# A mixture-of-experts tail in five parts: rows gathered one place ahead, more buffers, and a scaling kept in program order

## The chip, the cores and the metric

The kernel runs on one core of a Trainium2 chip. The metric is the device time of one execution in microseconds (us). Before the change it is 2043.39 us, the median of 3 runs (2043.01 to 2043.95).

A core has a matrix engine (TensorE, PE in the profile), a vector engine (VectorE, DVE), an engine for activation functions (ScalarE, ACT), a general engine (GpSimd, POOL) and a sequencer that here issues most of the transfers (SyncE, SP). Each works through its own list of instructions in order and waits on semaphores for the others. Matrix products land in PSUM, of which this kernel uses eight banks; everything else is in SBUF or in the chip's main memory.

## What is computed

Two layers on a tensor of 4 sequences of 512 positions of 512 features, all in 32-bit floats. Each layer adds an attention and a mixture of experts to its normalised input. The change lies in the second layer ("layer 1"), whose mixture is

```python
logits = einsum('bsd,de->bse', x, router_w) + router_b
topk_vals, topk_idx = top_k(logits, 2)
topk_w = softmax(topk_vals)
h = einsum('td,edf->etf', xf, expert_w) + expert_b
combined = sum over the two chosen experts of topk_w * silu(h)
out = combined @ proj_w + proj_b
y = x + out
return norm_w * y / sqrt(mean(y * y) + 1e-6)
```

and the layer's result is `x + attention(xn) + mixture(xn)`. Only the two experts chosen for a position count, so the kernel sorts the positions by expert, computes each expert on its own rows, and gathers every position's two rows back.

## The kernel before

The 2048 positions are 16 tiles of 128 rows. Layer 1's attention has 16 steps `g` (4 sequences times 4 groups of heads), each of 4 parts `kc` (128 keys each); a pair (g, kc) is called a place, and place number 4 g + kc runs from 0 to 63. In each place the loop at the end of `two_layers` writes, in this order:

- the scores (`weights`: TensorE L1322, then two exponentials on ScalarE, L1324);
- the weighted values of the place before (`attend`: TensorE L1336) and, for kc > 0, the running sums of the exponentials (VectorE L1342);
- for kc = 1 the sums over keys (`sum_keys`, L1350) and after it reciprocals (`invert`, L1360) and the scaling of the context (L1368);
- for kc < 2 the next step's queries and keys (`queries7`, L1298 and VectorE L1303 to L1313), and for kc > 1 in some steps the next sequence's values;
- `bring(n, 0)`, which reloads the partial result of a tile of an earlier sequence, and for kc = 3 that tile's output projection (`output1`, TensorE L1405), whose sum is added to it (`add_part`, VectorE L1394) and stored;
- then the jobs that a table (`jobs1`) has for this place.

Those jobs fill TensorE's time in the attention with the mixture: the routing first, the expert products in places 13 to 45 (`apply`, L529, whose result rows go to a table `yd` in main memory), and from place 48 on the last stage, which this change is about. Tile n starts at place 48 + 13 n // 16, so some places (48, 52, 56) start two tiles, and the last ends in place 63. A tile has four jobs in four places that follow each other:

- `mix`: two gathers from `yd` (`gather`, GpSimd issues them, L545) into `row0` and `row1`; the load of the normalised input `xnd` into a buffer `xr` (SP, L1435); the rows' weighted sum on VectorE (L1438, L1439); the bias `pb` added to the input on GpSimd (L1440).
- `turn_mix`: four transposes on TensorE (L1447), the reload of the tile's partial result from `accd` (`bring(n, 1)`, SP, L1390), the copy out of PSUM on ScalarE (L1451).
- `project_mix`: eight matmul records on TensorE (L1458), the sum with the input on VectorE (L1459), the squares on ScalarE (L1462), mean and power on GpSimd (L1463, L1464).
- `finish_mix`: the scaling with the norm's weight on VectorE (L1469), the addition to the partial result (L1394) and the store.

All buffers of this stage are in a pool `mix` with two buffers to a name. Products and transposes of the stage take their PSUM bank from the same three (`bank1`, name `mm`) as the queries, the output projection and the key sums.

The order in which an engine executes is not the written one. A planner goes through the program with estimated times and gives each engine, of what is ready, the instruction written first; a tile that finds no free buffer is not ready. `tc.keep_in_program_order(instruction)` pins an instruction behind the one that was written last before it on its engine. In the stage only L1438 of the first two tiles is pinned.

## Time and profile before

| | |
|---|---|
| median of 3 runs | 2043.39 us |
| profiled execution | 2039.16 us |
| its span, first to last instruction | 2037.1 us |
| TensorE busy in the span | 1983.6 us (97%) |
| VectorE busy | 1506.5 us (74%) |
| GpSimd busy | 746.3 us (37%) |
| last stage, place 48 to the last weighted values | 1860.6 to 2012.8 us of the span |

The profile is of one execution. A row of the stretch view gives the stretch and its length, then the busy time of each engine with the number of instructions, then the clock granted to TensorE as a share of full speed, the busy share of the transfer engines and their rate. A row of the view of waits gives the engine, the tile and line that waited, what ended the wait, and then the sum in us, how many times, and the longest. A row of the view in order of time gives start, duration, engine, line, operation, output and inputs, and in brackets the idle time of the engine before it with its releaser.

### The profile page before, as it was taken

What the parts mean: (1) busy time and instruction counts of PE and PEld (TensorE: products, weight loads), DVE (VectorE), ACT (ScalarE), POOL (GpSimd) and SP (SyncE); (2) the same over time, 40 slices, a digit from 0 to 9 for tenths busy, and PEclk for the clock granted to TensorE, in tenths of its full rate; (3) what the DMA queues carried; (4) which work ended last, traced back from release to release, by engine and by line L of the source; (5) the groups of instructions that cost most, each with busy time, mean ns of one, the idle gap of its engine ahead of it and who ended that gap; (6) DMA issues with size and microseconds to landing.
All of it is one profiled execution on the core that took longest, in us unless ns stands there. A gap on an engine that the chain in (4) does not pass through costs nothing.

```text
span 2037.1 us, 28573 instructions
## 1 busy us (share of the span) xinstructions
PE 1983.6 (97%) x9358; PEld 1243.6 (61%) x9358; DVE 1506.5 (74%) x3696; ACT 868.5 (43%) x2600; POOL 746.3 (37%) x761
## 2 busy tenths in 40 slices
PE   7999999999999999999999999999999999999998
PEld 4666667777777777767667666666334445445443
DVE  7889968777776777786678878788596555557775
ACT  4554444444444444444444454454244432332332
POOL 4423144443323333344343444353114332322550
PEclk8999999999999999999999999999999999999999
DMA  7101133333433343245443222121317775773551
GB/s 254 69 33 62 43 120 123 145 109 114 126 133 104 115 153 104 96 135 186 183 161 118 73 89 74 42 74 64 121 55 253 271 255 194 270 245 112 154 161 59
DMA packets 98909, 267.27 MB, mean 131 GB/s; under 512 B 14400, under 2 KB 27840, under 8 KB 87488
## 3 DMA queue, kind: packets, MB, share of 16 engines
q0 software_dynamic: 27072, 148.91, 21.6%
q1 hardware_dynamic: 70528, 114.34, 16.7%
q10 hardware_dynamic: 1152, 2.10, 0.3%
q8 instruction: 77, 1.26, 0.3%
q14 instruction: 80, 0.66, 0.1%
HBM read 222.05 MB, written 42.73 MB: 130 GB/s over the span
## 4 chain that ended last, share of the span: by engine, by line
PE 81%; DVE 9%; ACT 3%; POOL 2%; issue 2%; DMA 1%; ACTq 0%; DVEq 0%; SPq 0%; POOLq 0%
PE p L675 25%; PE hp_r L529 12%; PE op L842 4%; PE st L767 4%; PE sp L758 2%; PE st L1322 2%; PE ox L873 2%; PE qp L1298 2%; PE cx L1336 2%; PE ca L811 2%; DVE pS L1342 2%; PE o L1405 2%; PE oz L873 2%; PE trm_r L517 1%; PE trq L695 1%
## 5 line engine op out<-in xcount | busy, mean ns | idle before, releaser
L529 PE MATMUL hp_r<-we_r,xT_r 128*128 128x512 f32 (+1 forms) x592 | 224.7, 596 | 2.7 <-ACT xT_r L519 2.2
L481 POOL DMA_INDIRECT xr_r<-xnd,rows_r x72 | 87.5, 1216 | 342.2 <-PE trm_r L517 299.0
L775 POOL TENSOR_TENSOR lT<-lT,lmask 128x512 f32<-128x512 f32 (+1 forms) x128 | 152.6, 1200 | 129.1 <-ACT lT L771 128.9
L675 PE MATMUL p<-wT,x 128*128 128x384 f32 x512 | 178.7, 492 | 0.8 <-DVE wT L119 0.8
L675 PE MATMUL p<-wB,x 128*128 128x384 f32 x512 | 176.2, 488 | 3.0 <-DVE u L731 3.0
L675 PE MATMUL p<-wA,xnT 128*128 128x384 f32 x512 | 174.3, 492 | 0.3 <-DVE u L710 0.2
L575 ACT ACTIVATE sq<-qb 128x128 f32<-128x128 f32 x384 | 118.9, 310 | 96.2 <-DVE qb L724 45.8
L1324 ACT ACTIVATE pT<-st 128x1024 f32<-128x1024 f32 x128 | 123.3, 1014 | 62.5 <-PE st L1322 56.7
L529 PEld LDWEIGHTS hp_r<-we_r,xT_r 128*128 128x128 f32 (+1 forms) x592 | 83.0, 170 | 98.8 <-issue 92.5
L675 PEld LDWEIGHTS p<-wB,x 128*128 128x128 f32 x512 | 93.7, 190 | 67.1 <-issue 9.6
L675 PEld LDWEIGHTS p<-wA,xnT 128*128 128x128 f32 x512 | 95.5, 193 | 61.6 <-issue 3.3
L675 PEld LDWEIGHTS p<-wT,x 128*128 128x128 f32 x512 | 94.2, 192 | 62.7 <-issue 5.5
L689 ACT ACTIVATE qb<-qb,ss 128x128 f32<-128x128 f32 x256 | 81.9, 390 | 106.6 <-POOL ss L578 104.5
L519 ACT COPY xT_r<-trm_r 128x512 f32<-128x512 f32 x72 | 41.9, 581 | 193.4 <-PE hp_r L529 180.8
L767 PE MATMUL st<-qkT 128*128 128x256 f32 (+1 forms) x512 | 114.7, 354 | 1.5 <-ACT qkT L702 1.5
L771 ACT ACTIVATE lT<-st,ss 128x256 f32<-128x256 f32 (+1 forms) x128 | 49.0, 446 | 153.0 <-PE st L767 153.0
L545 POOL DMA_INDIRECT row_r<-yd,slot_r x64 | 75.0, 1172 | 89.8 <-DVE row_r L1439 37.6
L767 PEld LDWEIGHTS st<-qkT 128*128 128x128 f32 x512 | 92.2, 190 | 11.9 <-ACT qkT L702 1.7
L578 POOL TENSOR_TENSOR ss<-ss,nhalf 128x6 f32<-128x6 f32 x64 | 95.4, 1490 | 5.3
L842 PE MATMUL op<-Wo,cT 128*128 128x512 f32 x208 | 93.7, 595 | 0.4 <-DVE lv L739 0.4
L577 POOL TENSOR_SCALAR ss<-ss 128x6 f32<-128x6 f32 x64 | 31.0, 485 | 164.3 <-ACT sq L575 163.9
L675 PE MATMUL p<-wT,xnT 128*128 128x384 f32 x256 | 88.0, 486 | 0.0
(384 smaller groups left out, 4632.7 us busy)
## 6 DMA issues: line engine op xcount, KB each, us to landing
x<-xsd SPq DMA_DIRECT2D x112, 256.0 KB, 3.2
yd<-yr_r SPq DMA_DIRECT2D x72, 256.0 KB, 4.4
wA<-in_wA SPq DMA_DIRECT2D x16, 384.0 KB, 3.9
wB<-in_wB SPq DMA_DIRECT2D x16, 384.0 KB, 7.6
xnd<-xn SPq DMA_DIRECT2D x24, 256.0 KB, 2.1
accd<-acc SPq DMA_DIRECT2D x18, 256.0 KB, 2.0
acc<-in_x SPq DMA_DIRECT2D x16, 256.0 KB, 4.9
Wo<-in_Wo SPq DMA_DIRECT2D x8, 512.0 KB, 3.7
```

The lines of the kernel that those rows point to most:

```text
L481: G.indirect_dma_start(out=out, out_offset=None, in_=src, in_offset=at_rows(idx))
L529: PE.matmul(hp[ts(h, m), :], lhsT=xT[:, k, ts(h, m)], rhs=w[:, ts(k, HID)], start=(k == 0), stop=(k == KC - 1))
L545: G.indirect_dma_start(out=x, out_offset=None, in_=self.yd, in_offset=at_rows(self.r.slot[:, k, n : n + 1]))
L575: A.activation(sq, x[:, h, :], AF.Square, accum_out=ss[:, h : h + 1])
L578: pin(G.tensor_tensor(ss, ss, nhalf[:, 0:n], ALU.pow))
L675: PE.matmul(p, lhsT=x[:, k, ts(c, P)], rhs=w[:, k, :], start=(k == 0), stop=(k == 1))
L689: A.activation(x[:, j, :], x[:, j, :], AF.Copy, scale=sq[t][:, j : j + 1])
L767: PE.matmul(st[:, ds((t % 2) * 256, n)], lhsT=qkT[:, HG + h, ts(t, P)], rhs=qkT[:, h, ds(t * P, n)], start=True, stop=True)
L775: G.tensor_tensor(dst, dst, lmask.rearrange("p a w j -> p (a w j)")[:, 0:n], ALU.mult)
L842: PE.matmul(op, lhsT=cT[:, h, ts(t, P)], rhs=wo[:, h, :], start=(h == 0), stop=(h == HG - 1))
L873: PE.matmul(p[:, ts(c, 256)], lhsT=left[:, ts(c, P)], rhs=right, start=new and c == 0, stop=True, skip_group_check=True)
L1324: A.activation(pt[:, ts(pair, 2), :], st, AF.Exp, scale=SCALE1)
```

## The change

The stage has five jobs instead of four. The gathers become a job of their own, `fetch_mix`, one place ahead of `mix`, and the pool of the stage is opened one place earlier (place 47). `row0` has four buffers and `row1` three in this layer, `xr` four, the transposed tile (`xT`) three, the squares (`th`) one. The load of `xnd` moves from `mix` to `turn_mix`, the addition of `pb` from `mix` to `project_mix`. L1438 is pinned for all tiles, and so is L1469. The reload for the output projection, `bring(n, 0)`, is written in kc = 0 instead of kc = 1.

```diff
--- before.py
+++ after.py
@@ -541,7 +541,8 @@
 
             rs = []
             for k in range(2):
-                x = self.pool.tile([P, HID], F32, tag=f"row{k}", name=f"row{k}_{self.r.name}_{n}")
+                x = self.pool.tile([P, HID], F32, tag=f"row{k}", name=f"row{k}_{self.r.name}_{n}",
+                                   bufs=(4, 3)[k] if self.silu else None)
                 G.indirect_dma_start(out=x, out_offset=None, in_=self.yd,
                                      in_offset=at_rows(self.r.slot[:, k, n : n + 1]))
                 rs.append(x)
@@ -1428,36 +1429,38 @@
         for nm in ("pb", "nw1"):
             rows[nm] = load(rout["mix"], nm, [P, HID], a[nm].partition_broadcast(P))
 
+    def fetch_mix(n):
+
+        held[n] = rout["ex1"].gather(n)
+
     def mix(n):
 
-        g0, g1 = rout["ex1"].gather(n)
-        x = rout["mix"].tile([P, HID], F32, tag="xr", name=f"xa_{n}")
+        g0, g1 = held[n]
+        tc.keep_in_program_order(V.tensor_scalar(g0, g0, r1.gate[:, 0, n : n + 1], None, ALU.mult))
+        V.scalar_tensor_tensor(g0, g1, r1.gate[:, 1, n : n + 1], g0, ALU.mult, ALU.add)
+        held[n] = g0
+
+    def turn_mix(n):
+        g0 = held[n]
+        x = rout["mix"].tile([P, HID], F32, tag="xr", name=f"xa_{n}", bufs=4)
         nc.sync.dma_start(out=x, in_=xnd[ts(n, P), :])
-
-        pin = tc.keep_in_program_order if n < 2 else (lambda x: x)
-        pin(V.tensor_scalar(g0, g0, r1.gate[:, 0, n : n + 1], None, ALU.mult))
-        V.scalar_tensor_tensor(g0, g1, r1.gate[:, 1, n : n + 1], g0, ALU.mult, ALU.add)
-        G.tensor_tensor(x, x, rows["pb"], ALU.add)
-        held[n] = g0, x
-
-    def turn_mix(n):
-        g0, x = held[n]
         tr = bank1("mm", f"trc_{n}")
         for f in range(KC):
             PE.transpose(tr[:, ts(f, P)], g0[:, ts(f, P)], ident)
         bring(n, 1)
-        cT_ = rout["mix"].tile([P, KC, P], F32, tag="xT", name=f"combT_{n}")
+        cT_ = rout["mix"].tile([P, KC, P], F32, tag="xT", name=f"combT_{n}", bufs=3)
 
         A.activation(cT_, tr.rearrange("p (k t) -> p k t", k=KC), AF.Copy, scale=0.5)
         held[n] = cT_, x
 
     def project_mix(n):
         cT_, y = held.pop(n)
+        G.tensor_tensor(y, y, rows["pb"], ALU.add)
         op = bank1("mm", f"po_{n}")
         for f in range(KC):
             PE.matmul(op, lhsT=cT_[:, f, :], rhs=wa["pw"][:, f, :], start=(f == 0), stop=(f == KC - 1))
         V.tensor_tensor(y, y, op, ALU.add)
-        sq = rout["mix"].tile([P, HID], F32, tag="th", name=f"ysq_{n}")
+        sq = rout["mix"].tile([P, HID], F32, tag="th", name=f"ysq_{n}", bufs=1)
         ss = small.tile([P, 1], F32, tag="yss", name=f"yss_{n}")
         A.activation(sq, y, AF.Square, accum_out=ss)
         G.tensor_scalar(ss, ss, 1.0 / HID, 1e-6, ALU.mult, ALU.add)
@@ -1466,7 +1469,7 @@
 
     def finish_mix(n):
         y, ss = held.pop(n)
-        V.scalar_tensor_tensor(y, y, ss[:, 0:1], rows["nw1"], ALU.mult, ALU.mult)
+        tc.keep_in_program_order(V.scalar_tensor_tensor(y, y, ss[:, 0:1], rows["nw1"], ALU.mult, ALU.mult))
         add_part(n, y, 1)
 
 
@@ -1499,10 +1502,10 @@
             ex.fetch_bias(i + 2)
         jobs1.append((at[here], after))
     first += 6 + NS * 11 // 12
-    jobs1.append((at[first], begin_mixing))
+    jobs1.append((at[first - 1], begin_mixing))
     for n in range(NT):
         here = first + n * 13 // 16
-        for d, f in ((0, mix), (1, turn_mix), (2, project_mix), (3, finish_mix)):
+        for d, f in ((-1, fetch_mix), (0, mix), (1, turn_mix), (2, project_mix), (3, finish_mix)):
             jobs1.append((at[here + d], lambda n=n, f=f: f(n)))
 
     left_ = sums_qk()
@@ -1556,7 +1559,7 @@
             if kc > 1 and j + 1 == NJ and 1 < b + 1 < B:
                 values7(b + 1, kc - 2)
 
-            if kc == 1 and g > NJ:
+            if kc == 0 and g > NJ:
                 bring(g - NJ - 1, 0)
             if kc == 2 and g + 1 == NG:
                 bring(NT - TC - 1, 0)
```

## The prediction

> **What bounds the kernel now.** I read the page first, then the busy time of each engine in stretches of the last stage, then the waits of each queue there, and last its instructions in order of time. The page says that TensorE is the bound over the whole program: nothing can be gained where it is busy.

> ```profile
> span 2037.1 us, 28573 instructions
> PE 1983.6 (97%) x9358; PEld 1243.6 (61%) x9358; DVE 1506.5 (74%) x3696; ACT 868.5 (43%) x2600; POOL 746.3 (37%) x761
> ```

> The diff touches what runs in places 47 to 63 of layer 1. The score matmuls (L1322) that open a place put place 48 at 1860.6 us and place 63 at 2001.2 us. The stretch view (PE, PEld, DVE, ACT, POOL busy, granted clock, DMA share, GB/s) of that stage, and inside it of a quiet place and the two worst:

> ```profile
> 1860.60:2012.80 152.20, 142.85 (x613) 63.59 (x612) 110.42 (x154) 55.88 (x96) 70.64 (x74) 0.98 0.43 127
> ...
> 1935.00:1948.30 13.30, 11.29 (x45) 6.58 (x44) 8.80 (x13) 3.99 (x7) 6.81 (x8) 0.87 0.66 200
> 1948.30:1958.40 10.10, 10.10 (x57) 5.35 (x56) 7.24 (x12) 3.93 (x8) 5.67 (x7) 1.00 0.55 154
> ...
> 1978.50:1988.50 10.00, 7.85 (x29) 3.00 (x28) 6.21 (x7) 3.62 (x6) 4.93 (x5) 0.83 0.63 212
> ```

> In 152.2 us TensorE idles 152.20 - 142.85 = 9.35 us, and after its two long gaps the clock is down. That is all this change can win. TensorE's waits in the stage:

> ```profile
> PE qp L1298 <- DVE xnT L1394: 3.1, 2, 2.0
> PE po L1458 <- DVE acc L1394: 2.2, 1, 2.2
> PE trc L1447 <- DVE qk L1311: 1.3, 2, 1.0
> PE po L1458 <- DVE xa L1459: 0.9, 2, 0.5
> PE sm L1350 <- DVE pS L1342: 0.7, 1, 0.7
> PE cx L1336 <- ACT pT L1324: 0.5, 1, 0.5
> PE o L1405 <- DVE xa L1459: 0.5, 2, 0.3
> ```

> Nearly all are on VectorE, and mostly not for data: `qp`, `po`, `trc`, `o` take one of three PSUM banks of one tag, and the bank's last user has not been read out. Yet VectorE is only 110.42 of 152.2 us busy. It is late because it waits in order:

> ```profile
> DVE xa L1469 <- POOL yss L1464: 28.7, 14, 3.5
> DVE row_r L1438 <- DMA row_r<-yd,slot_r: 4.5, 6, 1.7
> ```

> ```profile
> POOL row_r L545 <- DVE row_r L1439: 37.6, 11, 10.5
> POOL xa L1440 <- DMA xa<-xnd: 21.1, 10, 4.8
> ```

> The last scaling of a tile (L1469) was put right behind that tile's projection sum (L1459), and holds VectorE until the sum of squares has gone through ScalarE and GpSimd. Behind the wait for the power stand GpSimd's gathers (L545), which wait for a row buffer (two of each), and its adds (L1440), which wait for a reload into one of two `xr` buffers. One turn of the loop, on VectorE:

> ```profile
> 1903.61 0.68 DVE L1459 TENSOR_TENSOR xa<-xa,po 128x512 f32<-128x512 f32 x1
> 1907.78 0.75 DVE L1469 SCALAR_TENSOR_TENSOR xa<-xa,yss,nw 128x512 f32<-128x512 f32 x1 [3.49 <-POOL yss L1464]
> ...
> 1909.40 0.49 DVE L1438 TENSOR_SCALAR row_r<-row_r,gate_r 128x512 f32<-128x512 f32 x1
> ```

> After these come sums and a reciprocal, and the key sums that free a bank for `trc` only at 1912.6 us; TensorE stood 1.02 us.

> **The change part by part.** No compute instruction and no transfer is added or removed; it moves them and orders them.

> **The pins.** L1469 is put behind what was written before it on VectorE, one place after L1459. Its power (0.19 + 0.56 us on GpSimd) then has a place of 6 to 13 us instead of none, so the 28.7 us of waiting go. Behind L1469 are queued the add that ends a tile (L1394), L1459 of the next tile and L1438/L1439 of the one after; TensorE waits for the bank that L1459 frees. L1438 is pinned behind L1459 of the tile two before, so VectorE now may idle there until TensorE ends `po`; `trc`, which needs L1439, comes a place later. That costs nothing while the pair (0.48 + 0.75 us) fits in a place; without that cover it is 1.2 us a tile.

> **The gathers.** 32 of them at 1.02 us median on GpSimd, 4.2 us median to landing: a round of 5.2 us. Written a place ahead, with four and three buffers for two and two, they wait for rows released at least a full place before. The 4.5 us of L1438 go; so does most of the 37.6 us, which are GpSimd's. GpSimd is at 70.64 of 152.2 us, and gathers pass in front of adds and powers: up to two gathers, 2 us, ahead of a power that now has a place to spare. At the start nothing moves: the first four already ran at 1845.6 to 1850.8 us.

> **The `xa` load, SP's queue.** 16 loads (0.32 us to issue, 3.4 us to landing) go from the mixing place to the transposing one, four buffers. They now stand just ahead of the tile's reload of `accd`, which holds SP for an earlier output store (28.4 us in 9 waits, 4.0 at most). 4.0 + 3.4 us are less than all places but the short ones (5.7 us).

> **The `pb` add (L1440)** goes two places on, next to L1459: 16 x 1.28 us, the same work, but cover is gone. If late it delays L1459, that bank, then TensorE. From below 0; from above the whole 21.1 us that GpSimd waits for these loads today. I take 2.0 us with the pins' own lateness: nearest are today's waits on a late L1459, 0.9 + 0.5 us.

> Four `xr`, three `xT` and one `th` buffer (its writer, ScalarE, is in order with itself) cost nothing, nor does the reload for the attention output one place up: its row shows it issued as soon as the store ahead of it has landed.

> [...] After the gap of 2.01 us at 1937.1 the next eight `qp` matmuls take 3.68 instead of 1.99 us, and after that of 2.15 us at 1980.7 eight `po` take 5.37 instead of 3.60; the granted clock reads 0.50 for about 3 us each time. [...]

> **The sum.** Four gaps behind a late VectorE, 1.12 + 1.02 + 2.01 + 2.15 = 6.3 us; the clock after two, 3.5; half of the four small ones where two projections meet three banks (0.25 + 0.47 twice = 1.44), 0.7; half of the tail's 0.53 + 0.68, 0.6, as ScalarE's exponentials stood 4.65 us behind a late square there; less new waits, 2.0. 6.3 + 3.5 + 0.7 + 0.6 - 2.0 = 9.1 us, say 9.0. The profiled execution took 2039.16 us (span 2037.1, 2.06 around it), so 2030.2; it lies 4.2 us under the median of the runs, and the difference carried over gives 2043.4 - 9.0 = **2034.4 us** (own range 2030.5 to 2039.3; without the clock's part 2037.9).

> **Rivals.** **All of it:** idle time and clock wholly recovered, 9.35 + 3.5 = 12.9 us, 2030.5 us. For it: each wait begins in VectorE's two wait rows. Against: `trc` behind L1311 in place 49 (0.25 us) has no scaling ahead of it, and the two-projection places stay crowded.
> **Nothing:** the order of what is not pinned (sums, projection sums, gathers) is still planned from estimated times; VectorE then waits on rows or on `po` rather than on powers, and the banks come as late. 2043.4 us, within 4 us. Against: 33 us of VectorE's waits lose their cause.
> **Slower:** the `pb` add comes late to L1459. Mechanism: GpSimd in order, a gather waiting for L1439, or a load behind SP's reload, ahead of the add; L1459 is held, then a bank. If all ten waits of today (21.1 us) pass on to TensorE in full: + 21.1 - 12.9 = 8.2 us, 2051.6 us. It decides from 12.9 / 16 = 0.8 us of new TensorE idling a tile.

> **How the numbers follow.** Forecast 0.55, all of it 0.15, nothing 0.14, slower 0.16. About 0.2% (4 us) is what a measurement of this kernel tells from no change, so faster 0.70, same 0.14, slower 0.16. Low: 2029.5, an us under full recovery, since nothing else of TensorE's time is touched. High: 2048, which takes in "nothing" and leaves out most of "slower".

> **What would show it.** L1469's wait for `yss` falls from 28.7 us to under 5; L1438's for rows to about 0; `qp` and `po` no longer wait for L1394; TensorE idles under 4 us between places 48 and 63 and the clock stays at 1.00 there; GpSimd's gathers hardly wait for L1439. The forecast is wrong if L1459 shows a wait for L1440, or TensorE new waits on L1459 of more than 5 us together, or if VectorE's pinned order makes the sums (L1342) late, so that ScalarE and the score matmuls wait.

## The result, and the profile after

The changed kernel takes **2026.85 us** (median of 4 runs, 2026.39 to 2027.63) against 2043.45 us for the kernel before in the same comparison (2043.01 to 2043.95). The ratio is **0.9915, 95% interval 0.9903 to 0.9927**: 16.6 us faster. The direction was right. The size was not: 9.0 us were forecast, and the time lies below the low end of the range, 2029.5 us.

The profiled execution of the changed kernel took 2026.99 us. Its page says that TensorE is now busy for 98% of the span:

```profile
span 2025.2 us, 28527 instructions
PE 1976.5 (98%) x9358; PEld 1241.0 (61%) x9358; DVE 1509.9 (75%) x3696; ACT 870.4 (43%) x2600; POOL 746.8 (37%) x761
```

The gain lies in two stretches. The first runs from the scores of place 48 to those of place 63, the second ("the tail") from there to the last output projection, behind the last key sums. The stretch view of the kernel before (stretch and length, then PE, PEld, DVE, ACT and POOL busy, clock, transfer share, rate):

```profile
1860.60:2001.20 140.60, 132.54 (x573) 60.82 (x572) 101.05 (x143) 52.22 (x91) 69.90 (x72) 0.98 0.46 137
2001.20:2012.82 11.62, 10.33 (x41) 2.77 (x40) 9.37 (x12) 3.65 (x6) 0.74 (x2) 1.00 0.01 2
```

The same two stretches after, and then both together:

```profile
1864.20:1992.40 128.20, 127.95 (x573) 59.49 (x572) 105.94 (x145) 52.22 (x91) 65.24 (x69) 1.00 0.43 140
1992.44:2000.66 8.22, 8.22 (x42) 2.49 (x41) 7.00 (x9) 3.14 (x5) 0.74 (x2) 1.00 0.01 2
1864.23:2000.66 136.43, 136.18 (x614) 61.98 (x613) 112.98 (x153) 55.36 (x96) 65.95 (x71) 1.00 0.41 131
```

The places give 140.6 - 128.2 = 12.4 us and the tail 11.62 - 8.22 = 3.4 us, together 15.8 us. In 136.43 us TensorE now idles 0.25 us. Almost all that is left here is the work of TensorE itself; only the last key sums still take 1.71 us where the others of this kernel take 1.04.

The waits of the changed kernel in the stage, by engine and line, read from 1845 to 2013 us as those of before were (L1439 and L1440 are now the weighting, L1458 the `pb` add, L1462 the projection's sum, L1467 the power, L1472 the last scaling):

```profile
POOL row_r L546 <- PE trc L1449: 12.0, 6, 4.4
POOL xa L1458 <- DMA xa<-xnd: 11.8, 8, 3.8
POOL row_r L546 <- DVE row_r L1440: 6.4, 2, 6.1
DVE xa L1462 <- PE po L1461: 2.3, 4, 1.2
DVE xa L1472 <- POOL yss L1467: 1.6, 2, 0.9
PE trc L1449 <- DVE qk L1312: 0.2, 1, 0.2
```

VectorE's 28.7 us for the power are 1.6, its 4.5 us for rows are gone from the list, TensorE waits 0.2 us for VectorE, and the gathers' 37.6 us behind the weighting are 6.4. GpSimd still waits for the loads of `xnd` (11.8 us), but no row has VectorE waiting for the `pb` add.

In order of time the scaling stands one place behind its projection's sum (that of this tile starts at 1884.93 us), with no idle time in front (no bracket in its row):

```profile
1892.37 0.69 DVE L1395 TENSOR_TENSOR xnT<-xnT,o 128x512 f32<-128x512 f32 x1 [1.18 <-PE o L1406]
1892.98 0.74 DVE L1472 SCALAR_TENSOR_TENSOR xa<-xa,yss,nw 128x512 f32<-128x512 f32 x1
```

### The profile page after: what moved, and what is told of

It is laid out like the page before. It is cut to its first block, busy times and chain, and to the rows that moved or that the text cites. A ratio compares the mean times of both kernels' runs of the same rounds, so it can differ in the third digit from the quotient of the medians.

```text
span 2025.2 us, 28527 instructions
## 1 busy us (share of the span) xinstructions
PE 1976.5 (98%) x9358; PEld 1241.0 (61%) x9358; DVE 1509.9 (75%) x3696; ACT 870.4 (43%) x2600; POOL 746.8 (37%) x761
## 4 chain that ended last, share of the span: by engine, by line
PE 85%; DVE 7%; ACT 2%; POOL 2%; issue 1%; DMA 1%; ACTq 0%; DVEq 0%; POOLq 0%
PE p L676 25%; PE hp_r L529 12%; PE op L843 4%; PE st L768 4%; PE st L1323 3%; PE po L1461 3%; PE cx L1337 3%; PE sp L759 3%; PE ox L874 2%; PE qp L1299 2%; PE o L1406 2%; PE ca L812 2%; PE oz L874 2%; PE trq L696 1%; PE trm_r L517 1%
```

## The experiments

Three theories stood at the start. **The pin:** L1469's wait is the root of the others, so the pin of the last scaling brings most of the gain. **The rows:** early gathers and more row buffers bring it. **The interlock:** VectorE works in order and waits for whatever is latest, so a part that cures one wait only lets it stand at the next one. The parts were tried one at a time on the kernel before, and taken away one at a time from the kernel after.

The stage's length below is from the scores of place 48 to the last output projection behind the key sums, in one profiled execution of each kernel (before: to 2012.82 us; the last weighted values themselves start at 2008.06 us). Ratios are to the kernel before on the same chip.

| kernel | ratio, 95% interval | stage, us |
|---|---|---|
| before | 1 | 152.2; second profile 153.1 |
| before + pin of the last scaling | 1.0056 [1.0039, 1.0072] | 163.2 |
| before + that pin + four `xr` | 0.9993 [0.9984, 1.0002] | 150.6 |
| before + early rows, row buffers, pinned weighting | 0.9991 [0.9982, 1.0000] | 151.2 |
| before + all of these four parts | 0.9915 [0.9901, 0.9929] | 136.42 |
| before + early rows, row buffers, weighting not pinned | 1.0059 [1.0042, 1.0076] | 154.8 (and 12.3 more in place 47) |
| after | 0.9915 [0.9903, 0.9927] | 136.43 |
| after, last scaling not pinned | 0.9971 [0.9960, 0.9983] | 147.3 |
| after, load and add in `mix`, two `xr` | 0.9953 [0.9937, 0.9970] | 142.0 |
| after, load and add in `mix`, four `xr` | 0.9909 [0.9893, 0.9926] | 136.42 |
| after, two row buffers | 0.9946 [0.9930, 0.9963] | 140.2 |
| after, weighting pinned for two tiles only | 1.0048 [1.0031, 1.0065] | 149.3 (and 14.3 more in place 47) |
| after, `bring(n, 0)` in kc = 1 | 0.9904 [0.9887, 0.9920] | 136.5 |

### The pin of the last scaling alone

```diff
-        V.scalar_tensor_tensor(y, y, ss[:, 0:1], rows["nw1"], ALU.mult, ALU.mult)
+        tc.keep_in_program_order(V.scalar_tensor_tensor(y, y, ss[:, 0:1], rows["nw1"], ALU.mult, ALU.mult))
```

> The kernel before with one thing of the change: the last scaling (L1469) pinned in program order. Theory P (VectorE is late because the scaling stands before it waits for its power; before: 28.7 us in 14 waits): VectorE's waits for yss go under 8 us, and most of the 16.6 us come, 2033 us or less. Theory B (it is late because rows and xr buffers come back late; before: GpSimd waits 37.6 us for L1439 and 21.1 us for xa loads): the waits move to L1438 on rows and the time stays at 2039 us or more. Theory E (both loops hold it, each as long as the other is there): 2034 to 2039 us.

Measured: 2053.42 us, ratio 1.0056 [1.0039, 1.0072], 11 us **slower**. Its waits in the stage (L1440 is the `pb` add here):

```profile
DVE row_r L1438 <- DMA row_r<-yd,slot_r: 17.0, 6, 4.2
DVE xa L1459 <- POOL xa L1440: 14.8, 3, 6.3
PE po L1458 <- DVE xa L1459: 9.5, 2, 5.3
```

In order of time, the worst of them:

```profile
1904.71 0.69 DVE L1459 TENSOR_TENSOR xa<-xa,po 128x512 f32<-128x512 f32 x1 [6.29 <-POOL xa L1440]
1905.45 6.27 PE L1458 MATMUL po<-pw,combT 128*128 128x512 f32 x8 [4.25 <-DVE xa L1459]
```

The wait for the power is gone (3.7 us are left), and worse ones stand in its place. The scaling comes a place later, so `y`, which is the `xr` buffer, comes back later. With two of them the next load starts later, the `pb` add behind it too, L1459 waits for the add, and the bank that L1459 should free holds TensorE up for 9.5 us. The eight `po` after the long gap take 6.27 instead of 3.6 us. The pin theory falls in this form; theory B's time came, with 17.0 us of waiting for rows and a late `xr` buffer.

### The pin with four `xr` buffers

On top of the pin, still on the kernel before:

```diff
-        x = rout["mix"].tile([P, HID], F32, tag="xr", name=f"xa_{n}")
+        x = rout["mix"].tile([P, HID], F32, tag="xr", name=f"xa_{n}", bufs=4)
```

> The kernel before with the last scaling pinned and four xr buffers, load and pb add left in the mixing job, rows as before. Theory H (the pin alone lost because the later finish gave back two xr buffers later, so that L1459 waited 14.8 us for the pb add): L1459's waits for GpSimd go to under 2 us and the time is 2036 us or less. Theory R (rows in two buffers hold it as well; pin alone: 17.0 us of L1438 for rows): 2037 to 2046 us with L1438's wait still over 10 us.

Measured: 2040.85 us, ratio 0.9993 [0.9984, 1.0002], about no change. L1459 no longer waits for the `pb` add, which shows the chain of the last run from its other end. What VectorE waits for now are rows:

```profile
DVE row_r L1438 <- DMA row_r<-yd,slot_r: 27.9, 9, 4.9
```

In order of time, one such wait and what came of it:

```profile
1912.42 0.59 DVE L1438 TENSOR_SCALAR row_r<-row_r,gate_r 128x512 f32<-128x512 f32 x1 [4.89 <-DMA row_r<-yd,slot_r]
...
1916.90 1.09 PE L1447 MATMUL trc<-ident,row_r 128*128 128x128 f32 x8 [2.38 <-DVE qk L1311]
```

That is the turn of the loop shown before, with another wait at its head: the weighting waits 4.89 us, the sums that free a bank are queued behind it, and TensorE stands 2.38 us. The wait for the power (28.7 us) has become a wait for rows (27.9 us), as theory R had it.

### Early rows with a pinned weighting, last scaling as before

On the kernel before:

```diff
+                                   bufs=(4, 3)[k] if self.silu else None)
...
+    def fetch_mix(n):
+        held[n] = rout["ex1"].gather(n)
...
-        pin = tc.keep_in_program_order if n < 2 else (lambda x: x)
+        pin = tc.keep_in_program_order
...
-    jobs1.append((at[first], begin_mixing))
+    jobs1.append((at[first - 1], begin_mixing))
...
-        for d, f in ((0, mix), (1, turn_mix), (2, project_mix), (3, finish_mix)):
+        for d, f in ((-1, fetch_mix), (0, mix), (1, turn_mix), (2, project_mix), (3, finish_mix)):
```

> The kernel before with the gathers one place ahead, four and three row buffers, and L1438 pinned for all tiles; last scaling and xr as before. Theory H: the wait of 9.5 us in place 47 is gone, so at least 10 us under the gathers alone (2055.4 us); about 2041 to 2045 us, since VectorE still waits some 28 us for the powers. If the rows themselves held the kernel before, 2037 us or less.

Measured: 2040.1 us, ratio 0.9991 [0.9982, 1.0000]. The rows are there in time: the wait for them is gone from the list of the stage's waits. The power takes its place in full (L1474 is the last scaling here):

```profile
DVE xa L1474 <- POOL yss L1469: 29.5, 14, 4.6
```

So the rows theory falls too; the time lies an us under the 2041 to 2045 us of theory H. One half of the change turns the wait into one for rows, the other half keeps the one for the power. Each half alone is worth 0.1% or nothing.

### The four parts together

Both halves on the kernel before: the pin of the last scaling, four `xr`, early rows with four and three buffers, the weighting pinned for all tiles. The load of `xnd`, the `pb` add and `bring(n, 0)` stay where they were, `xT` and `th` keep two buffers. The diff is that of the last three sections together.

> The kernel before with four parts of the change and nothing else: the last scaling pinned, four xr buffers, the gathers a place ahead into four and three row buffers, the first weighting pinned for all tiles. The load of the input and the pb add stay in the mixing place, the reload for the output projection in kc = 1, xT and th with two buffers. Theory of the interlock (these four are the whole change): 2025.2 to 2027.6 us, ratio 0.9905 to 0.9917 to the kernel before; the wait for the power under 3 us, no wait of the projection sum for GpSimd over 2 us, the weighting's wait for rows under 2 us. Rival (the load and the add only may stay where they were because of the third xT buffer or of the reload moved up; with none of these the transposes or the copy wait): 2028.5 to 2034 us, with a wait of ScalarE's copy for an xT buffer, or of the projection's matmuls for the copy, of 3 us or more.

Measured: 2025.31 us, ratio 0.9915 [0.9901, 0.9929], the time of the whole change. The waits on VectorE that the halves left are gone together:

```profile
POOL xa L1445 <- DMA xa<-xnd: 15.5, 9, 3.8
DVE xa L1474 <- POOL yss L1469: 1.6, 2, 0.9
```

The stage takes 136.42 us, the changed kernel's 136.43. The two halves gain 0.07% and 0.09% alone and 0.85% together. That is the interlock, and it is shown; the waits of the rival did not appear.

### Each part taken from the whole

**Without the pin of the last scaling** (the diff of the first experiment the other way round):

> The changed kernel without the pin of the last scaling. Theory P: 2037 us or more, and VectorE again waits over 15 us for yss. Theory B: at most 2031 us, since a scaling that waits only for ScalarE and an unblocked GpSimd (some 2 us a tile) is small. Theory E: 2031 to 2037 us.

Measured: 2036.7 us, ratio 0.9971 [0.9960, 0.9983]. The wait for the power is back:

```profile
DVE xa L1472 <- POOL yss L1467: 26.2, 14, 4.9
```

The wait is that of theory P, the time lies just under P's 2037 us, in the range of E. So this one edit is worth 0.9971 - 0.9915 = 0.56%, some 11 us, with the other parts in place, and -0.56% without them.

**Load and add in `mix` again, two `xr` buffers:**

```diff
@@ mix
+        x = rout["mix"].tile([P, HID], F32, tag="xr", name=f"xa_{n}", bufs=2)
+        nc.sync.dma_start(out=x, in_=xnd[ts(n, P), :])
+        G.tensor_tensor(x, x, rows["pb"], ALU.add)
@@ turn_mix
-        x = rout["mix"].tile([P, HID], F32, tag="xr", name=f"xa_{n}", bufs=4)
-        nc.sync.dma_start(out=x, in_=xnd[ts(n, P), :])
@@ project_mix
-        G.tensor_tensor(y, y, rows["pb"], ALU.add)
```

> The changed kernel with the xa load and the pb add back in the mixing job and two xr buffers. Theory P: the pins keep GpSimd's lateness off VectorE, so at most 2030 us, with GpSimd's waits for xa loads near the 21.1 us of before. Theory B: the xr loop (load, add, scaling, next load) takes back 4 us or more, 2031 us or over.

Measured: 2031.5 us, ratio 0.9953 [0.9937, 0.9970]. The projection's sum waits for GpSimd's add, as with the pin alone:

```profile
DVE xa L1462 <- POOL xa L1443: 10.6, 5, 3.1
```

**The same with four `xr` buffers** (`bufs=4` in the first line of that diff):

> The changed kernel with the xa load and the pb add back in the mixing job, but with four xr buffers. The same with two buffers gave 2031.5 us and VectorE waited 10.6 us for the pb add. Theory K (the number of buffers counts, not the place where load and add are written): at most 2028 us, with under 3 us of that wait. Theory L (the place counts: a load that is written two places earlier needs its buffer two places earlier, four are too few): 2030 us or more.

Measured: 2026.16 us, ratio 0.9909 [0.9893, 0.9926], as fast as the whole. No row has L1462 waiting for the add. The number of buffers does the work. With four of them, where the load and the add are written does nothing, and the two steps of the prediction that priced those moves priced something that costs nothing here. Two buffers with the load and the add at their new places were not tried.

**Two row buffers instead of four and three** (the `bufs` of the row tile left out):

> The changed kernel with two row buffers each, as before. Theory R (a pinned L1438 must have its rows early): VectorE waits 10 us or more for rows, 2033 us or more. If the pin of the last scaling and the xr buffers are what counts: 2030 us or less.

Measured: 2030.1 us, ratio 0.9946 [0.9930, 0.9963]. The time lies between those of the two theories. The rows are late again, for 5.9 us where theory R had 10 or more, and the kernel before 4.5:

```profile
DVE row_r L1438 <- DMA row_r<-yd,slot_r: 5.9, 3, 3.1
```

**The weighting pinned for two tiles only, as before the change:**

```diff
-        tc.keep_in_program_order(V.tensor_scalar(g0, g0, r1.gate[:, 0, n : n + 1], None, ALU.mult))
+        pin = tc.keep_in_program_order if n < 2 else (lambda x: x)
+        pin(V.tensor_scalar(g0, g0, r1.gate[:, 0, n : n + 1], None, ALU.mult))
```

> The changed kernel with L1438 pinned only for the first two tiles, as before the change. Theory H (a row buffer more lets the planner put the weighting of a third tile into place 47, ahead of rows that have not landed, as the run with the gathers alone showed with 9.5 us of waiting): the same wait of 5 to 10 us for rows in place 47 and 2034 to 2040 us. Theory N (with the last scaling pinned the order comes out right anyway): 2029 us or less.

Measured: 2052.06 us, ratio 1.0048 [1.0031, 1.0065], slower than the kernel before. Without this pin the change loses 1.3%, more than it brings. In order of time, VectorE in place 47 (L1440 is the weighting here):

```profile
1849.96 0.69 DVE L1265 TENSOR_TENSOR xnT<-vp,xnT 128x512 f32<-128x512 f32 x1 [0.43 <-PE vp L1259]
1860.69 0.49 DVE L1440 TENSOR_SCALAR row_r<-row_r,gate_r 128x512 f32<-128x512 f32 x1 [10.03 <-DMA xa<-xnd]
```

With a third row buffer free, the planner finds the third tile's weighting ready, by its estimate, and puts it on VectorE a place early, between two steps that build the next values (L1265 and L1266). The rows are not there. VectorE stands 10 us (the profile names the load that landed last; in the next run but one the same wait is put down to the rows), TensorE's `vp` products wait for L1266, and place 47 lasts 25.2 us instead of the usual 10.9. In the stage itself the weighting then waits another 25.7 us for rows, so that the time lies 12 us over the highest that theory H allowed. The wait in place 47 is that of H.

**The reload back in kc = 1:**

```diff
-            if kc == 0 and g > NJ:
+            if kc == 1 and g > NJ:
```

> The changed kernel with the reload for the output projection written in kc = 1 again. Theory of the prediction (the reload already goes out as soon as the store ahead of it has landed): no difference, 2025 to 2029 us, and its issues within a few us of those of the changed kernel. Theory F (SP's queue needs it early): 2030 us or more.

Measured: 2025.39 us, ratio 0.9904 [0.9887, 0.9920]. This move does nothing, as the prediction had it.

### Early rows and more buffers, without any new pin

The third diff above without its line on `pin`, on the kernel before.

> The kernel before with the gathers one place ahead and four and three row buffers, and the stage's pool opened in place 47; no pins, xr as before. Theory P: VectorE still waits over 20 us for yss, 2039 us or more. Theory B: 2035 us or less. The 4.5 us in which VectorE waited for rows should be gone in either.

Measured: 2055.4 us, ratio 1.0059 [1.0042, 1.0076]. The time is as theory P had it, but the wait for rows, which should have been gone under either theory, is 10.6 us. It is the same trap as with the weighting pinned for two tiles only, on the other kernel (L1443 is the weighting here):

```profile
1851.66 0.69 DVE L1265 TENSOR_TENSOR xnT<-vp,xnT 128x512 f32<-128x512 f32 x1 [0.43 <-PE vp L1259]
1861.82 0.49 DVE L1443 TENSOR_SCALAR row_r<-row_r,gate_r 128x512 f32<-128x512 f32 x1 [9.47 <-DMA row_r<-yd,slot_r]
1862.22 0.68 DVE L1266 TENSOR_TENSOR xnT<-vp,xnT 128x512 f32<-128x512 f32 x1
```

Place 47 takes 23.2 us. Against the run with the pinned weighting (0.9991, place 47 at 10.9 us) only the pin differs, so the 0.7% between them are the pin's.

### The kernel before, profiled again

No edit. The profiled execution shown at the start lay 4.2 us under the median, and this was to show where.

> The kernel before, unchanged, for a second profile. Theory C (the spread of its runs, 2039.4 to 2046.1 us, is whether the clock halves after its gaps of about 2 us): the same gaps in the last stage, but another number of halved stretches, each worth 1.7 us. Theory S (it lies in the part of the program ahead of place 48): place 48 starts some 3 us later than at 1860.6 us, as it did in all profiles of the variants (1862.8 to 1864.2 us).

Measured: 2044.48 us. The stretches from place 48 to place 63, and from there to the end of the span:

```profile
1864.69:2005.85 141.16, 131.22 (x574) 60.26 (x573) 100.66 (x143) 51.78 (x91) 71.28 (x72) 0.99 0.45 136
2005.85:2042.30 36.45, 28.60 (x82) 10.20 (x82) 18.68 (x32) 4.68 (x8) 0.74 (x2) 0.96 0.13 47
```

Place 48 starts at 1864.69 us, not at 1860.6, and close to the changed kernel's 1864.23. So 4.1 us of the first execution's advance lay ahead of the stage (theory S), and carrying them over was right. Theory C holds as well: of two like gaps (2.01 and 2.07 us) only the first was followed by a halved clock here, where both (2.01 and 2.15 us) were in the first profile. From place 48 on this execution takes 141.16 + 36.45 = 177.6 us, the changed kernel 2025.2 - 1864.23 = 161.0: 16.6 us, the gain between the medians.

## Why the prediction was right in its direction and wrong in its size

**The step that failed** is "In 152.2 us TensorE idles 152.20 - 142.85 = 9.35 us, and after its two long gaps the clock is down. That is all this change can win." Idle time and clock, 12.9 us, were taken as the ceiling, and the low end of the range stood on it ("since nothing else of TensorE's time is touched"). The medians moved by 16.6 us, the stretches in the two traces by 15.8. The same 573 matmuls of the places were busy 132.54 us before and 127.95 after, 4.6 us less, where the clock's part of the sum is only 3.5. In the tail the busy time of nearly the same matmuls (41 and 42 records) fell by another 2.1 us, with the clock at 1.00 throughout. So waiting was booked as work. The tail, before, with two rows of the weight loads (PEld) that go ahead of the `cx` matmuls:

```profile
2001.24 1.66 PE L1322 MATMUL st<-qk 32*128 32x512 f32 x8
...
2008.05 0.14 PEld L1336 LDWEIGHTS cx<-pT,v 128*32 128x32 f32 x4 [1.35 <-ACT pT L1324]
2008.06 1.97 PE L1336 MATMUL cx<-pT,v 128*32 128x512 f32 x8 [0.53 <-ACT pT L1324]
2008.97 0.14 PEld L1336 LDWEIGHTS cx<-pT,v 128*32 128x32 f32 x4 [0.77 <-ACT pT L1324]
2010.70 2.19 PE L1350 MATMUL sm<-pS,ones 128*32 128x512 f32 x8 [0.68 <-DVE pS L1342]
```

and after:

```profile
1992.44 1.14 PE L1323 MATMUL st<-qk 32*128 32x512 f32 x8
...
1998.14 0.20 PEld L1337 LDWEIGHTS cx<-pT,v 128*32 128x32 f32 x8 [0.76 <-ACT pT L1325]
1998.14 1.10 PE L1337 MATMUL cx<-pT,v 128*32 128x512 f32 x8
1999.02 1.71 PE L1351 MATMUL sm<-pS,ones 128*32 128x512 f32 x8
```

The same eight matmuls take 1.66 and 1.14 us, 1.97 and 1.10, 2.19 and 1.71. The length of a single one did not change. The rows of the `cx` tile, with least, median and longest record in ns, before and after:

```profile
L1336 PE MATMUL cx<-pT,v x16: 592/605/617, 2002.8 to 2009.4; 128*32 128x512 f32 x16
```

```profile
L1337 PE MATMUL cx<-pT,v x16: 592/605/617, 1993.5 to 1998.7; 128*32 128x512 f32 x16
```

Eight records of 0.6 us that take 1.10 us together overlap: the four heads run side by side (after, one record of each starts between 1998.14 and 1998.20 us). Before, the weight loads show that the second pair of heads waits for the second exponential until 2008.97 us, while records of the first pair still run, to 2009.11 us. TensorE works on half of its heads and counts as busy, so the wait shows as a longer group and not as idle time. The three groups are longer by 0.52 + 0.87 + 0.48 = 1.87 us, most of the tail's 2.1. In the places the 1.1 us (4.6 - 3.5) sit in groups directly behind a stop: 0.24 us in each of two `po`, 0.22 in two `trc`, 0.07 in two `o` and one `qp`. Without a stop a group starts while the record before it still runs, and that overlap is lost behind a stop: in the changed kernel `po` starts at 1930.91 us, 0.16 us before the record ahead of it ends at 1931.08.

**The sum, term by term.** The four gaps (6.3 us) and the clock (3.5) came back in full. The halves taken of the two-projection gaps (0.7) and of the tail's (0.6) should have been the whole, 1.44 and 1.21: TensorE idles 0.25 us in the places and not at all in the tail (ScalarE still waits 5.05 us for the late square there, but the square now comes 3.15 us after the scores of place 63 instead of 5.13). That makes 12.4, and with the 1.1 and 2.1 us of hidden waiting 15.6, against 15.8 in the two stretches (the second profile of before has the remaining 0.8). "Less new waits, 2.0" measured nothing: no row has L1462 waiting for the `pb` add or TensorE for L1462. Against "9.1" the terms are off by 2.0 (new waits), 1.4 (halves) and 3.2 (hidden waiting).

**The pins.** "The 28.7 us of waiting go" was right: 1.6 are left. That the pinned weighting costs nothing fits too, as TensorE's 0.25 us of idling leaves no room for a cost. What was not seen is that the change fails without this pin. The prediction asked what it might cost, and not what the planner does with the new buffers if it is missing.

**The gathers.** The weighting no longer waits for rows, and "at the start nothing moves" held for this kernel, because the pin held the third weighting back. The two runs without it lost 9.5 and 10 us at just that place.

**The `xa` load and the `pb` add.** With four buffers both moves cost nothing, and gain nothing. Four `xr` buffers instead of two are worth 0.9953 - 0.9909 = 0.44%, with load and add in `mix`, and the prediction had booked them as costing nothing and named no gain.

**The clock and VectorE's rows.** Taking the clock's part from the rows, 3.68 - 1.99 and 5.37 - 3.60 us, was right; these 3.5 us came back with the gaps. VectorE's busy time in the stage rose, from 110.42 to 112.98 us. The rows that got longer, after; behind the first bar stand busy us and mean ns of one (before: 752, 690 and 1211 ns):

```profile
L1472 DVE SCALAR_TENSOR_TENSOR xa<-xa,yss,nw 128x512 f32<-128x512 f32 x16 | 13.7, 856 | 1.7 <-POOL yss L1467 1.6
L1395 DVE TENSOR_TENSOR acc<-acc,xa 128x512 f32<-128x512 f32 x14 | 10.7, 766 | 0.3
L1343 DVE TENSOR_TENSOR pS<-pT,pT 128x1024 f32<-128x1024 f32 x8 | 11.5, 1436 | 1.8 <-PE sm L1351 1.8
```

The weighting's second half got shorter instead, 875 to 741 ns. In all VectorE is busy 2.6 us longer than before. The moved adds are not the whole cause: with the adds in `mix` VectorE is busy 111.62 us in the stage of the four parts, and 113.19 us in that of early rows with a pinned weighting. What lengthens the rows is shown for one of them only, in the last section. None of it reached TensorE, since VectorE still has 136.43 - 112.98 = 23 us to spare in the stage.

**The rivals.** "All of it" (2030.5) came nearest, and missed by what the idle time does not show. "Slower" by a late `pb` add was no fancy: the pin alone brought it about, with L1459 late by 14.8 us, held up by an `xr` buffer that came back late. That its time of 2053.4 us lies near the 2051.6 worked out is luck: those were for another edit, with another sum. Four buffers keep it away. "Nothing" is what each half alone gives (0.9993 and 0.9991). With the pin and four `xr` it is for the reason given there, VectorE "then waits on rows" rather than on powers; with the early rows the powers simply stay.

## What to carry to other kernels

Where an in-order engine waits for several late things in turn, cure them together, or you may measure nothing: two halves worth 0.1% each made 0.85%. Where buffers are added or an instruction is pinned, ask what now lives longer and what a planner may now hoist, because the same edit was worth +0.56% of time or -0.56% by its neighbours. And the idle time that the trace of before showed between TensorE's overlapping matmuls was 3.2 us short of its waiting: compare the length of like groups of instructions in two traces.

## What the runs showed of the hardware

```profile
1935.79:1939.20 3.41, 1.40 (x13) 0.25 (x9) 3.41 (x5) 0.00 (x0) 1.60 (x1) 1.00 0.73 228
1939.20:1942.61 3.41, 3.41 (x8) 2.71 (x9) 0.45 (x1) 2.86 (x5) 3.07 (x5) 0.50 0.68 172
```

The second profile, where a gap of 2.07 us lies across the start of a step, at 1984.66 us, and leaves 3.41 - 1.48 = 1.93 us of idling in it:

```profile
1984.66:1988.07 3.41, 1.48 (x4) 0.79 (x5) 2.39 (x4) 0.93 (x3) 1.32 (x2) 1.00 0.68 240
1988.07:1991.48 3.41, 3.41 (x18) 1.46 (x16) 1.44 (x2) 2.69 (x4) 1.73 (x3) 1.00 0.90 281
```

The same holds, from 1840 to 2019 us, in the six traces with halved stretches there (both of before, the pin alone, early rows with and without a pinned weighting, the weighting pinned for two tiles only): all eleven steps at full clock in which TensorE idled 2.00 us or more (2.00 to 3.41) were followed by a halved one, and of those with 1.98 us or less a single one was (1.78 us, in the run with the pin alone). A gap of 3.08 us cost no clock (changed kernel without the pin of the last scaling: 1.00 from its end at 1960.28 to 1966.28 us); one of 2.00 us inside a step did (weighting pinned for two tiles only). So much the same gap ahead of eight `po`, 2.15 and 2.07 us, made them take 5.37 us in the first profile of before and 3.67 in the second. It may be part of why runs of the kernel before spread over 2039.4 to 2046.3 us and the four of the kernel after, which has no such gap, over 2026.4 to 2027.6; that was not tested.

**One collision.** VectorE's first key sum takes 1.21 us in the mean before. Beside GpSimd's add it once took 2.94 us (changed kernel, in order of time):

```profile
1947.60 2.94 DVE L1343 TENSOR_TENSOR pS<-pT,pT 128x1024 f32<-128x1024 f32 x1 [0.36 <-PE sm L1351]
1948.16 1.28 POOL L1458 TENSOR_TENSOR xa<-xa,pb 128x512 f32<-128x512 f32 x1
1949.61 1.77 POOL L546 DMA_INDIRECT row_r<-yd,slot_r  x1 [0.16 <-issue]
```

The add's 1.28 us and the gather behind it, itself longer than the 1.02 us median before, fall inside or against the sum's 2.94 us. Which held which the rows do not show. In the run with the weighting pinned for two tiles only, a sum that starts at 1863.39 us took 5.33 us.

**Left open.** Whether a pin of the third tile's weighting alone would do in place of one on all tiles was not tried, nor were the added row buffers without the gathers a place ahead: what each of these two is worth by itself is not shown. No version was found that beats the changed kernel by more than the measurement can tell: the four parts alone are as fast, with TensorE equally full.
